# Local attention: softmax division moved ahead of the transposes, weighted values made feature by token, and a new order table

## The chip, the cores and the metric

The kernel runs on one core of one Trainium2 chip. The metric is device time in microseconds (us) of one execution. The core has five engines with in-order instruction queues: TensorE (PE, with its weight loads shown as PEld), VectorE (DVE), ScalarE (ACT), GpSimd (POOL) and SyncE (SP), which only issues DMAs here. They meet through semaphores.

## The reference

Four stages follow each other on an input of 4 sequences of 512 tokens with 128 features: a gated scan with a short convolution, a mixture of eight experts of which one is chosen, grouped-query causal attention, and a stack of six layers of local attention with a gated feed-forward. Only the last stage is touched by the change. One of its layers is, in the reference:

```python
qkv = x @ Wqkv                                   # 16 heads of 64 features
q = l2norm(q) * qs;  k = l2norm(k) * ksc         # then rotary tables with scale
sim = einsum('bhwie,bhwje->bhwij', bq, bk2) * 8  # 32 queries against 64 keys
sim = where(mask, -max, sim)
attn = softmax(sim, -1)
out = einsum('bhwij,bhwje->bhwie', attn, bv2)
return out.reshape(b, n, 1024) @ Wo
...
x = attn_layer(shift_tokens(x), ...) + x
x = ffn_layer(shift_tokens(x), ...) + x
```

Windows have 32 queries, and each window sees its own 32 keys and the 32 before them.

## The kernel before, in words

**Tiling.** The last stage works on chunks of 128 tokens: 6 layers x 4 sequences x 4 chunks = 96 chunks. `Chunk` (class at L531) holds the steps of one. `query(j)` makes 512 columns of queries (j = 0, 1) or keys (j = 2, 3) as [token, feature] in PSUM (L550) and their squares on ACT (L555). `squares` sums these by head (L575). `rotate` multiplies by the two rotary tables on DVE (L563, L567) and adds the products on POOL (L572). `norms` takes the power -0.5 on POOL (L586), and `scale_keys` applies it to the keys on POOL (L593). `turn(j)` transposes four 128x128 blocks on PE (helper at L141) and copies the result to `qT` or `kT` (helper `move`, L529). `values` makes the values (L603, copied by ACT at L607 to a `vr` tile with 65 columns a head, the last of them ones). `spread` issues the DMAs that lay the values of each window's 64 keys into the four `vk` tiles (L617 to L621).

**Scores and softmax.** `mask` writes the mask into the PSUM tile `S` with a bfloat16 matmul (L643), and `scores(g)` adds 32 small matmuls for each half of the heads: 64 rows of features, 32 queries as weights, 64 keys as moving columns (L655). `largest` takes the negative maximum per head and query (L666) and multiplies it by the query's norm (L670). `exponentials(g)` runs four activations of 64 columns each (L679). `flip(g)` transposes half of the exponentials (L689) to `lpT`.

**Weighted values.** `weigh(g)` runs 32 small matmuls for half of the heads with the transposed exponentials as weights (64 keys x 32 queries) and `vk` as 65 moving columns (L702). The result is [token, feature], and its 65th column is the sum of the exponentials. `divide(g)` takes the reciprocal of that column (L711) and multiplies (L713) into `on`. `lift(j)` transposes `on` by four 128x128 blocks (L141, seen as tp_on) and copies it to `oT`. `project` multiplies by the output weights (L729) and adds into the residual (L735).

**Order.** The order of work is written out by hand. `TURN` is a table of (lag, step, arguments). Turn i runs every row on chunk i - lag, so one turn carries one step of each kind, for up to four chunks. `FEED` says ahead of which row of which turn one piece of the feed-forward (a generator with eight pieces per sequence and layer) is put in. `COPIES` says for each of four turns whether a copy out of PSUM goes to DVE ("v") or ACT ("a"). At the end a dependency chains every instruction to the one before it on its engine, so each engine runs exactly this order.

**Buffers.** PSUM has two tiles each of tags "mm" and "tr", and one each (of two banks) of "S" and "o". `qT`, `lp` and `lpT` have one buffer, `vr` has two. A small float32 matmul is one row in the program and two weight loads with two matmuls in the trace.

Of the kernel before, what the change touches and what calls it, by code (L numbers as in the profile page):

```python
# [8 lines left out]
F32 = mybir.dt.float32  # L9
# [6 lines left out]
P = 128  # L16
# [51 lines left out]
def fused(ctx: ExitStack, tc: tile.TileContext, a: dict, out: bass.AP):  # L68
# [387 lines left out]
    with ExitStack() as stage:  # L456
# [21 lines left out]
        vr = [sp.tile([P, 2, HEADS // 2, DH + 1], F32, name=f"vr{i}") for i in range(2)]  # L478
        vk = [sp.tile([P, HEADS // 2, DH + 1], F32, name=f"vk{i}") for i in range(NB)]
        for v in vr:  # L480
            nc.vector.memset(v[:, :, :, DH : DH + 1], 1.0)
# [49 lines left out]
        class Chunk:  # L531


            def __init__(self, n, l, b, c, w, last):
                self.l, self.b, self.c, self.w, self.last = l, b, c, w, last
                self.tag = f"{l}_{b}_{c}"
                self.xs = sA[b][:, c * P : (c + 1) * P]
                self.V = vr[n % 2]
                self.ss = sm.tile([P, 2 * HEADS], F32, tag="ss", name=f"ss{self.tag}")
                self.q = {}  # L540
                self.sq = {}
                self.rot = {}
                self.o = {}
                self.on = {}
# [56 lines left out]
            def values(self, j):  # L601
# [6 lines left out]
                    self.V[:, :, 4 * j : 4 * j + 4, 0:DH],  # L608
# [14 lines left out]
            def window(self):  # L623

                self.qT = wk.tile([P, HEADS // 2, P], F32, tag="qT", name=f"qT{self.tag}", bufs=1)
# [36 lines left out]
            def largest(self):  # L662

                S = self.S.rearrange("p a (s k) -> p a s k", k=KB)
                m = sm.tile([P, HEADS // 2, 2], F32, tag="lm", name=f"lm{self.tag}")
                nc.vector.tensor_reduce(  # L666
                    m.rearrange("p s a -> p a s"), S, AX.X, ALU.max, negate=True
                )
                self.nb = sm.tile([P, HEADS], F32, tag="lnb", name=f"lnb{self.tag}")
                nc.vector.tensor_tensor(  # L670
                    self.nb, m.rearrange("p s a -> p (s a)"), self.rq, ALU.mult
                )
                self.P = wk.tile([P, HEADS, KB], F32, tag="lp", name=f"lp{self.tag}", bufs=1)
                self.pT = wk.tile([P, HEADS // 2, P], F32, tag="lpT", name=f"lpT{self.tag}", bufs=1)

            def exponentials(self, g):

                for i in range(4 * g, 4 * g + 4):
                    nc.scalar.activation(  # L679
                        self.P[:, i, :], self.S[:, i % 2, i // 2 * KB : (i // 2 + 1) * KB], AF.Exp,  # L680
                        bias=self.nb[:, i : i + 1], scale=self.rq[:, i : i + 1],
                    )

# [11 lines left out]
            def weigh(self, g):  # L695
                o = psum("o", f"lo{self.tag}_{g}")[:, :, 0 : 4 * (DH + 1)]
                self.o[g] = o = o.rearrange("p a (s d) -> p a s d", s=4)
                for i in range(4):
                    for r in range(NB):
                        for par in range(2):  # L700
                            lo, to = par * KB, r * QB
                            nc.tensor.matmul(  # L702
                                o[to : to + QB, par, i, :],
                                lhsT=self.pT[lo : lo + KB, 4 * g + i, to : to + QB],
                                rhs=vk[r][lo : lo + KB, 4 * g + i, :], start=True, stop=True,
                            )

            def divide(self, g):
                gt, o = f"{self.tag}_{g}", self.o[g]
                r = sm.tile([P, 2, 4], F32, tag="lr", name=f"lr{gt}")  # L710
                nc.vector.reciprocal(r, o[:, :, :, DH])  # L711
                self.on[g] = wk.tile([P, 512], F32, tag="on", name=f"on{gt}")
                nc.vector.tensor_tensor(  # L713
                    self.on[g].rearrange("p (s a d) -> p a s d", s=4, a=2), o[:, :, :, 0:DH],
                    r[:, :, :, None].to_broadcast([P, 2, 4, DH]), ALU.mult,
                )

            def lift(self, j, engine):

                if j == 0:  # L720
                    self.oT = wk.tile([P, HEADS // 2, P], F32, tag="oT", name=f"oT{self.tag}")
                tp = transposed(chunks(self.on[j]), f"on{self.tag}_{j}")
                move(engine, self.oT[:, 4 * j : 4 * j + 4, :], chunks(tp))

            def project(self):

                y = psum("mm", f"ly{self.tag}")[:, 0:P]
                for j in range(INNER // P):
                    nc.tensor.matmul(  # L729
                        y, lhsT=self.w["o"][:, j, :], rhs=self.oT[:, j, :],  # L730
# [8 lines left out]
        def feedforward(l, b, w):  # L739
# [62 lines left out]
            (3, "exponentials", 3), (1, "scale_keys"), (1, "query", 1), (1, "squares", 0),  # L802
            (2, "turn", 0, "e4"), (1, "rotate", 1), (0, "query", 2), (0, "rotate", 2),
            (3, "flip", 1, "e7"), (2, "mask"), (3, "weigh", 0), (2, "scores", 0),
            (2, "scores", 1), (2, "values", 1), (3, "divide", 0), (3, "weigh", 1), (2, "largest"),
            (1, "squares", 1), (3, "divide", 1), (2, "exponentials", 0), (3, "lift", 0, "e0"),
            (1, "scale_queries"), (2, "values", 0), (0, "query", 3), (0, "squares", 2),
            (1, "window"), (1, "turn", 1, "e5"), (0, "rotate", 3), (3, "lift", 1, "e1"),
            (0, "squares", 3), (0, "query", 0), (2, "spread"), (1, "turn", 3, "e3"),
            (2, "exponentials", 1), (1, "turn", 2, "e2"), (0, "rotate", 0),  # L810
# [158 lines left out]
```

## Time and profile before

| | us |
|---|---|
| median of 3 runs (range) | 2576.98 (2571.02 to 2581.21) |
| the profiled execution's own time | 2581.88 |
| its span | 2580.1 |
| PE busy | 2239.3 (87% of the span) |
| DVE busy | 1923.6 (75%) |
| POOL busy | 1394.2 (54%) |
| ACT busy | 1333.5 (52%) |

The last stage runs from about 735 us to 2555 us of the span. The busy shares above are means over all stages; the last stage has its own. In the profile a row of a group gives the line, engine and operation, the tiles written and read, the count, then busy time and mean duration in ns, and then the idle time of the engine before these instructions with what ended it. Groups overlap where work is pipelined, so busy time is the better figure of the two for a sum. The chain is the sequence of work that ended last, followed back from the end; "issue" in it is time in which an engine waited for nothing that the profile shows.

### The profile page before, as it was taken

Reading aid. Unit: us, or ns where it says so; the run is one execution under the profiler, and the core shown is the slowest. Engines: PE = TensorE matmul, PEld = TensorE weight load, DVE = VectorE, ACT = ScalarE, POOL = GpSimd, SP = SyncE. Lnnn points to the kernel's source line nnn. Section 1 sums busy time; section 2 is a strip of 40 time slices with the busy share of each in tenths; the row PEclk is TensorE's granted clock in tenths of the full one; section 3 lists DMA queues with packets and bytes.
Section 4 is the critical chain, followed back from the end, with each engine's and each line's share of the span. In section 5 each row is a group of like instructions: output and inputs, shape, how many; then the busy total and the mean of one; then the engine's idle time right before and its main releaser. Section 6 shows DMA issues by size and latency. Waiting matters only on the chain.

```text
span 2580.1 us, 80423 instructions
## 1 busy us (share of the span) xinstructions
PE 2239.3 (87%) x33872; PEld 1485.8 (58%) x33968; DVE 1923.6 (75%) x4052; ACT 1333.5 (52%) x3203; POOL 1394.2 (54%) x1002
## 2 busy tenths in 40 slices
PE   3699988888879899989999999998999998989885
PEld 2466644554546566656666666665666665656552
DVE  6444456666759888888888888887888988888863
ACT  1111123233336566666676656666666666666542
POOL 2000011111148777776777777777677777777650
PEclk6699999999999999999999999999999999999997
DMA  6000000000002322232222312222222321212220
GB/s 197 1 1 1 1 1 1 1 1 1 1 7 75 93 60 58 66 92 59 56 66 54 106 51 66 52 71 84 59 60 66 93 66 51 65 50 67 56 55 24
DMA packets 85380, 131.11 MB, mean 51 GB/s; under 512 B 15894, under 2 KB 33564, under 8 KB 84124
## 3 DMA queue, kind: packets, MB, share of 16 engines
q1 hardware_dynamic: 82172, 122.87, 17.6%
q8 instruction: 268, 4.39, 0.7%
q10 hardware_dynamic: 2848, 3.10, 0.4%
q14 instruction: 92, 0.75, 0.1%
HBM read 25.82 MB, written 1.05 MB: 10 GB/s over the span
## 4 chain that ended last, share of the span: by engine, by line
PE 51%; DVE 10%; issue 6%; POOL 1%; ACT 1%; DMA 1%; SPq 0%; POOLq 0%; DVEq 0%; ACTq 0%
PE q L550 10%; PE ly L729 6%; PE lv L603 6%; PE tp_r L141 5%; PE lo L702 5%; PE ls L655 4%; PE tp_on L141 4%; PE fa L768 2%; PE lpt L689 2%; PE fy L778 2%; PE fg L757 2%; DVE lt L563 1%; DVE lt L567 1%; DVE on L713 1%; PE ls L643 1%
## 5 line engine op out<-in xcount | busy, mean ns | idle before, releaser
L572 POOL TENSOR_TENSOR ro<-lt,lt 128x512 f32<-128x512 f32 x384 | 483.5, 1269 | 158.3 <-DVE lt L567 130.0
L679 ACT ACTIVATE lp<-ls,lnb,rn 128x64 f32<-128x64 f32 x1536 | 482.4, 431 | 78.4 <-DVE lnb L670 77.9
L550 PE MATMUL q<-wqkv,sA 128*128 128x512 f32 x768 | 399.9, 603 | 2.8 <-ACT sq L555 1.5
L586 POOL TENSOR_TENSOR rk<-rk,neg_half 128x16 f32<-128x16 f32 x96 | 278.8, 2905 | 147.4 <-DVE rk L582 144.6
L586 POOL TENSOR_TENSOR rn<-rn,neg_half 128x16 f32<-128x16 f32 x96 | 278.9, 2905 | 146.9 <-DVE rn L582 138.5
L563 DVE TENSOR_TENSOR lt<-q,rot 128x512 f32<-128x512 f32 x384 | 262.5, 684 | 72.4 <-ACT sq L555 61.6
L607 ACT COPY vr<-lv 128x512 f32<-128x512 f32 x192 | 113.6, 592 | 388.6 <-PE lv L603 388.2
L555 ACT ACTIVATE sq<-q 128x512 f32<-128x512 f32 x384 | 235.1, 612 | 137.0 <-PE q L550 116.6
L141 PEld LDWEIGHTS tp_r<-ident,ro 128*128 128x128 f32 x1536 | 186.5, 142 | 164.8 <-issue 114.8
L567 DVE TENSOR_TENSOR lt<-q,rot 128x512 f32<-128x512 f32 x384 | 260.8, 679 | 0.0
L575 DVE TENSOR_REDUCE ss<-sq 128x8 f32<-128x512 f32 x384 | 259.6, 676 | 0.0
L702 PEld LDWEIGHTS lo<-vk,lpT 64*32 64x32 f32 x12288 | 143.3, 110 | 187.4 <-issue 153.8
L702 PE MATMUL lo<-vk,lpT 64*32 64x65 f32 x12288 | 183.5, 234 | 59.3 <-issue 36.3
L603 PE MATMUL lv<-wqkv,sA 128*128 128x512 f32 x384 | 220.9, 659 | 3.9 <-DVE lnb L670 2.2
L141 PE MATMUL tp_r<-ident,ro 128*128 128x128 f32 x1536 | 216.5, 274 | 8.9 <-POOL ro L572 7.6
L655 PE MATMUL ls<-kT,qT 64*32 64x64 f32 x12288 | 155.1, 226 | 72.6 <-issue 72.6
L593 POOL TENSOR_TENSOR ro<-ro,rk 128x512 f32<-128x512 f32 x192 | 196.1, 1042 | 7.5
L729 PE MATMUL ly<-oT,lwo 128*128 128x128 f32 x1536 | 188.9, 276 | 1.4 <-DVE lt L567 1.2
L729 PEld LDWEIGHTS ly<-oT,lwo 128*128 128x128 f32 x1536 | 182.2, 193 | 13.1 <-issue 10.6
L655 PEld LDWEIGHTS ls<-kT,qT 64*32 64x32 f32 x12288 | 134.1, 105 | 81.1 <-issue 80.2
L550 PEld LDWEIGHTS q<-wqkv,sA 128*128 128x128 f32 x768 | 127.3, 194 | 69.0 <-issue 49.4
L666 DVE TENSOR_REDUCE lm<-ls 128x16 f32<-128x1024 f32 x96 | 117.2, 1221 | 52.3 <-PE ls L655 51.4
(184 smaller groups left out, 3949.2 us busy)
## 6 DMA issues: line engine op xcount, KB each, us to landing
vk<-vr SPq DMA_DIRECT2D x576, 130.0 KB, 2.4
vk<-vr SPq DMA_DIRECT2D x336, 65.0 KB, 2.0
wqkv<-in_lwqkv_dram SPq DMA_DIRECT2D x6, 1536.0 KB, 7.0
ew<-in_ew_dram SPq DMA_DIRECT2D x16, 256.0 KB, 6.1
lwo<-in_lwo_dram SPq DMA_DIRECT2D x6, 512.0 KB, 8.8
lw<-in_lw_dram SPq DMA_DIRECT2D x6, 341.0 KB, 10.3
cst<-in_cst_dram ACTq DMA_DIRECT2D x1, 1028.0 KB
x_in<-in_x_dram ACTq DMA_DIRECT2D x4, 256.0 KB
```

The lines of the kernel that those rows point to most:

```text
L141: nc.tensor.transpose(tp[:, c * P : (c + 1) * P], i[:, c, :], ident)
L550: nc.tensor.matmul(q, lhsT=self.xs, rhs=self.w["qkv"][:, j * 512 : (j + 1) * 512], start=True, stop=True,)
L563: nc.vector.tensor_tensor(heads(t1), heads(q), cs[:, None, :].to_broadcast([P, 8, DH]), ALU.mult)
L567: nc.vector.tensor_tensor(swapped(t2), swapped(q)[:, :, ::-1, :], sn[:, None].to_broadcast([P, 8, 2, 32]), ALU.mult,)
L572: nc.gpsimd.tensor_tensor(self.rot[j], t1, t2, ALU.add)
L575: nc.vector.tensor_reduce(self.ss[:, j * 8 : j * 8 + 8], heads(self.sq[j]), AX.X, ALU.add)
L586: nc.gpsimd.tensor_tensor(r, r, neg_half.to_broadcast([P, HEADS]), ALU.pow)
L603: nc.tensor.matmul(v, lhsT=self.xs, rhs=self.w["qkv"][:, (4 + j) * 512 : (5 + j) * 512], start=True, stop=True,)
L655: nc.tensor.matmul(S[to : to + QB, par, s, :], lhsT=self.qT[lo : lo + 64, s, to : to + QB], rhs=self.kT[lo : lo + 64, s, to : to + KB], st ...
L679: nc.scalar.activation(self.P[:, i, :], self.S[:, i % 2, i // 2 * KB : (i // 2 + 1) * KB], AF.Exp, bias=self.nb[:, i : i + 1], scale=self. ...
L702: nc.tensor.matmul(o[to : to + QB, par, i, :], lhsT=self.pT[lo : lo + KB, 4 * g + i, to : to + QB], rhs=vk[r][lo : lo + KB, 4 * g + i, :], ...
L729: nc.tensor.matmul(y, lhsT=self.w["o"][:, j, :], rhs=self.oT[:, j, :], start=j == 0, stop=j == INNER // P - 1,)
```

## The change

The exponentials now also give their row sums (`accum_out`). `invert` takes the reciprocals of the sums on DVE, and the new `divide` multiplies the exponentials by them on POOL, before `flip`. `weigh` swaps its operands: `vk` (64 keys x 64 features) is the weights and `lpT` (32 queries) the moving columns. The result is [feature, token], so `lift` is only a copy and its transposes are gone; so are the ones in `vr` and the 65th column. Heads land in `oT` in another order, and the rows of `Wo` are laid out to match on the host. `qT`, `lp` and `lpT` get two buffers, `vr` three. `largest` is split in two rows, and `TURN`, `COPIES` and `FEED` are new.

```diff
-        vr = [sp.tile([P, 2, HEADS // 2, DH + 1], F32, name=f"vr{i}") for i in range(2)]
-        vk = [sp.tile([P, HEADS // 2, DH + 1], F32, name=f"vk{i}") for i in range(NB)]
-        for v in vr:
-            nc.vector.memset(v[:, :, :, DH : DH + 1], 1.0)
+        vr = [sp.tile([P, 2, HEADS // 2, DH], F32, name=f"vr{i}") for i in range(3)]
+        vk = [sp.tile([P, HEADS // 2, DH], F32, name=f"vk{i}") for i in range(NB)]
...
+            def bias(self, engine):
                 self.nb = sm.tile([P, HEADS], F32, tag="lnb", name=f"lnb{self.tag}")
-                nc.vector.tensor_tensor(
-                    self.nb, m.rearrange("p s a -> p (s a)"), self.rq, ALU.mult
-                )
+                engine.tensor_tensor(
+                    self.nb, self.m.rearrange("p s a -> p (s a)"), self.rq, ALU.mult
+                )
...
                         bias=self.nb[:, i : i + 1], scale=self.rq[:, i : i + 1],
-                    )
+                        accum_out=self.sum[:, i : i + 1],
+                    )
+
+            def invert(self, g):
+                r = self.sum[:, 8 * g : 8 * g + 8]
+                nc.vector.reciprocal(r, r)
+
+            def divide(self, g):
+                p = self.P[:, 8 * g : 8 * g + 8, :]
+                nc.gpsimd.tensor_tensor(
+                    p, p, self.sum[:, 8 * g : 8 * g + 8, None].to_broadcast([P, 8, KB]), ALU.mult
+                )
...
             def weigh(self, g):
...
+                if g == 0:
+                    self.o = psum("o", f"lo{self.tag}")
+                for i in range(2 * g, 2 * g + 2):
                     for r in range(NB):
...
+                        for odd in range(2):
+                            s = 2 * i + odd
+                            for par in range(2):
+                                lo, to = par * KB, (par ^ odd) * DH
+                                t0 = i * P + r * QB
+                                nc.tensor.matmul(
+                                    self.o[to : to + DH, odd, t0 : t0 + QB],
+                                    lhsT=vk[r][lo : lo + KB, s, :],
+                                    rhs=self.pT[lo : lo + KB, s, r * QB : (r + 1) * QB],
+                                    start=True, stop=True,
+                                )
+
+            def lift(self, odd, engine):
+
+                if self.oT is None:
+                    self.oT = wk.tile([P, 2, HEADS // 4, P], F32, tag="oT", name=f"oT{self.tag}")
+                move(engine, self.oT[:, odd], chunks(self.o[:, odd]))
...
         TURN = (
...
+            (1, "scale_keys"), (1, "rotate", 1), (1, "window"), (1, "squares", 1),
+            (2, "scores", 1), (2, "values", 1), (0, "query", 2), (3, "flip", 0, "e6"),
+            (2, "largest"), (2, "bias", nc.vector), (0, "rotate", 2), (0, "squares", 2),
+            (3, "spread"), (1, "scale_queries"), (3, "flip", 1, "e7"), (0, "query", 0),
+            (3, "weigh", 0), (0, "rotate", 0), (3, "weigh", 1), (2, "exponentials", 1),
+            (3, "lift", 1, "e1"), (3, "lift", 0, "e0"), (1, "turn", 3, "e3"), (0, "query", 3),
+            (2, "exponentials", 0), (1, "turn", 2, "e2"), (0, "rotate", 3), (0, "squares", 3),
+            (2, "invert", 0), (2, "exponentials", 2), (2, "exponentials", 3), (3, "project"),
+            (1, "turn", 0, "e4"), (0, "squares", 0), (1, "turn", 1, "e5"), (1, "values", 0),
+            (0, "query", 1), (2, "invert", 1), (2, "divide", 0), (1, "mask"), (2, "divide", 1),
+            (1, "scores", 0),
         )
         COPIES = {
-            "e0": "avva",
-            "e1": "aaav",
-            "e2": "vava",
-            "e3": "avav",
-            "e4": "aaav",
-            "e5": "aaav",
-            "e6": "vvvv",
-            "e7": "aaaa",
+            "e0": "aavv",
+            "e1": "vvvv",
+            "e2": "vvva",
+            "e3": "aaaa",
+            "e4": "avaa",
+            "e5": "vvva",
+            "e6": "aaaa",
+            "e7": "aava",
         }
-        FEED = {0: (0, 36), 1: (6,), 2: (0,), 3: (16, 28, 38, 38)}
+        FEED = {1: (2, 38), 2: (6, 9, 21, 23, 33), 3: (30,)}
...
+    wo = np.asarray(i["L1_ffn_Wo"]).reshape(DEPTH, HEADS // 4, 2, 2, DH, D).copy()
+    wo[:, :, 1] = wo[:, :, 1, ::-1].copy()
+    wo = wo.reshape(DEPTH, INNER, D)
```

## The prediction

> **What bounds the kernel now.** I read the page first, for which engine is full.
>
> ```profile
> PE 2239.3 (87%) x33872; PEld 1485.8 (58%) x33968; DVE 1923.6 (75%) x4052; ACT 1333.5 (52%) x3203; POOL 1394.2 (54%) x1002
> q8 instruction: 268, 4.39, 0.7%
> PE 51%; DVE 10%; issue 6%; POOL 1%; ACT 1%; DMA 1%; SPq 0%; POOLq 0%; DVEq 0%; ACTq 0%
> ```
>
> TensorE leads the chain, but these are means over four stages. So I took the busy times of a steady stretch of the last stage: from one piece of the feed-forward (gates, L757) to the same piece 19 sequences, or 76 chunks, later. The columns are span, then busy time (and count) of PE, PEld, DVE, ACT and POOL, the granted clock, DMA share and GB/s.
>
> ```profile
> 961.88:2357.92 1396.04, 1279.84 (x24587) 865.27 (x24663) 1183.42 (x2261) 906.77 (x2167) 1029.38 (x728) 0.98 0.25 66
> ```
>
> That is 18.4 us a chunk: PE works 16.8 of them, DVE 15.6, POOL 13.5, ACT 11.9. PE is the bound, with 1.5 us of idle time a chunk. What ends that idle time stands in the view of waits (who waits for whom: total us, times, longest):
>
> ```profile
> PE ls L655 <- issue: 72.6, 49, 2.5
> PE lo L702 <- issue: 36.3, 37, 2.2
> PE lo L702 <- DVE on L713: 20.9, 18, 5.2
> ```
>
> The largest is "issue", waiting for nothing that the profile shows, and only inside the two bursts of small matmuls. The chain of one turn (start, us, what) shows where:
>
> ```profile
> 1371.77 0.79 PE lo L702 x53
> 1372.56 1.27 PE ls L655 x77
> 1373.84 1.05 PE lv L603 x2
> 1374.89 0.63 PE lo L702 x37
> 1375.52 0.69 issue
> 1376.21 0.43 PE lo L702 x22
> 1376.64 0.58 PE tp_on L141 x4
> ```
>
> Most of these gaps lie within one of a multiple of 256 PE instructions apart (loads and matmuls counted: 511 from the one at 1341.7 to that at 1359.4, 767 to the one at 1376.2). The q8 row above has 268 packets in 4.39 MB, 16.4 KB each; PE's 67,840 instructions make 265 blocks of 256. In the trace the last q8 packet before such a gap mostly starts 2.2 to 2.9 us before the gap ends. So PE runs dry of instructions when it gets through a block faster than the next one comes.
>
> **The change, part by part.** These are the groups, shapes kept apart, that the prices come from:
>
> ```profile
> L141 PE MATMUL tp_on<-ident,on 128*128 128x128 f32 x768 | 128.8, 293 | 14.2 <-DVE oT L529 7.6 <-DVE on L713 3.7 <-issue 2.3
> L702 PE MATMUL lo<-vk,lpT 64*32 64x65 f32 x12288 | 183.5, 234 | 59.3 <-issue 36.3 <-DVE on L713 20.9 <-DMA vk<-vr 1.8
> L655 PEld LDWEIGHTS ls<-kT,qT 64*32 64x32 f32 x12288 | 134.1, 105 | 81.1 <-issue 80.2 <-POOL ro L572 0.4
> L729 PEld LDWEIGHTS ly<-oT,lwo 128*128 128x128 f32 x1536 | 182.2, 193 | 13.1 <-issue 10.6 <-ACT lp L679 2.0 <-ACT oT L529 0.4
> L593 POOL TENSOR_TENSOR ro<-ro,rk 128x512 f32<-128x512 f32 x192 | 196.1, 1042 | 7.5
> L713 DVE TENSOR_TENSOR on<-lo,lr 128x512 f32<-128x512 f32 x192 | 132.8, 692 | 6.7
> L397 ACT ACTIVATION_READ_ACCUMULATOR gp<-gs,gnb 128x1 f32 x128 | 25.3, 198 | 0.0
> ```
>
> *Transposes of `on`.* Eight a chunk go. The chain by line gives them 3.5% of 2580.1 us, 90.3 us, or 0.94 us a chunk on PE: -0.94. Their two copies stay, as copies of the result itself.
>
> *The burst of `weigh`.* The count stays: 128 pairs of load and matmul a chunk. Now 64 pairs take 0.79 us (chain above), 12.3 ns a pair, 1.58 us a chunk. Afterwards a load has 64 columns instead of 32, the matmul 32 moving columns instead of 65, on four 64x64 pieces of the array instead of eight of 64x32. No row has this shape. A load lasts 105 ns at 32 columns and 193 at 128, 0.92 ns a column, so 64 columns hold a piece for 59 ns. Moving columns go by in 0.84 ns (512 take 0.43 us), so 32 take 27 ns. Four pieces at work, loads behind matmuls as in L729 (0.112 us a pair, about one load), make 59/4 = 14.7 ns a pair, 1.88 us a chunk; load and matmul in turn make 86/4 = 21.5 ns, 2.75 us; the pace of the score burst (1.28 us for 128 pairs, 10 ns) makes 1.28. I take 1.88, as full-width rows overlap: +0.30 (-0.30 to +1.17). [...] If the load alone set the old burst too, its price would double to 24.7 ns a pair, +1.58 a chunk, and the forecast below would be 2546 instead of 2423. Against that, the score burst with equal loads runs at 10 ns, so 12.3 is not the load's own limit.
>
> *Where the bursts lie.* Before, 516 PE instructions come in one stretch of 4.0 us (half of `weigh`, both `scores`, a value matmul, half of `weigh`): wherever a block begins, one lies wholly inside. After, by the instruction order, the 256 of the scores and the 256 of `weigh` stand apart. Between them are 28 instructions of about 3.5 us on one side (value, two `query`, two `flip`) and 80 of about 6.5 us on the other. A block is too fast only if it begins within 28 instructions of where a burst does: 2 x 56/256 = 0.44 a chunk, at 0.8 us (half of the typical 1.6 us gap) 0.35 us. Now it is 108.9/96 = 1.13. So -0.78 (0 to -1.13). [...]
>
> *PE's waits for `on`, `oT` and `vk`.* 20.9 + 7.6 + 3.7 + 1.8 = 34.0 us, 0.35 a chunk, go with `on`. What PE waits for next is the copy of `lpT`, two rows later on the same engines. I keep half: -0.18 (-0.35 to 0).
>
> *`spread`.* Its ten DMAs a chunk (eight at a sequence's start) are 0.54 us apart on SP and land 2.0 to 2.4 us after issue, so 8 us after the last `weigh` frees `vk`. SP holds nothing else but the next layer's weights. Before, it waited for values made in the same turn; after, those are a turn old and the next `weigh` is a turn minus the burst away, 15 us. No cost.
>
> *DVE.* Two L713 (0.61 start to start) and two reciprocals (0.23) go, two reciprocals of 128x8 come (0.2 each), 14 of 32 copies fall to it instead of 13 (+0.15): 15.6 - 1.7 + 0.4 + 0.15 = 14.5 us. Now `invert` waits on DVE for exponentials; behind it stand the next chunk's norms, rotation and squares, 1.9 us, which POOL and then PE wait for. DVE has 2.3 us to spare for it in a turn of 16.8.
>
> *ACT.* 16 sums are read out: the L397 row says 198 ns busy, but in the timeline the next activation starts 0.09 us after it. 12 exponentials now take 3.67 us, so 16 take 4.9 and grow by 1.5 (0 to 3.2). ACT: 11.9 + 1.5 - 0.1 = 13.3 us. The one place it can reach PE is `S`: the next mask waits for the last exponential. Scores' end, maximum 1.22, bias 0.69, exponentials 6.4, some seven copies and squares of 0.5 between, mask and scores 1.7: 13.5 us, hidden in the turn, even with 1.7 more.
>
> *POOL.* Two divisions in L593's shape, 1.0 us each start to start: 13.5 + 2.0 = 15.5 us. They lie beside PE's 16.8, but the cover is thin: 1.3 us. Behind `divide` on POOL stands `scale_keys` (2.9 + 2.0 us), which the key transposes on PE wait for; they come half a turn later. If POOL falls behind, its time is the turn.
>
> *Second and third buffers* cost nothing. The ramp, about 2400 to 2555 us, I leave as it is.
>
> Sum a chunk: -0.94 + 0.30 - 0.78 - 0.18 = -1.60, a turn of 16.8 us. Times 96: -154 us. The profiled execution took 2581.9, so 2428; it lies 4.9 above the median of the runs, so **2423**.
>
> **The rivals.**
> *POOL and DVE set the turn.* POOL's waits now (L586 on DVE 144.6 and 138.5 us, L572 on DVE 130.0) are 4.3 us a chunk. They speak for a queue that is ahead and should shrink as PE speeds up, but in-order queues that wait for each other keep some. With half: 15.5 + 2.15 = 17.7, 0.7 saved, 2510.
> *Faster still.* No fetch gap left and the burst at 10 ns: 16.8 - 0.35 - 0.60 = 15.8, just over POOL's 15.5: 2332. For it: the score burst does run so. Against: everything must fit.
> *Slower: the new burst.* Its two row halves write the same PSUM bank, which they did not before[...]. No row here has such a pair. If they go one after the other, two pieces work at a time: 86/2 = 43 ns a pair, 5.5 us, +3.9 a chunk in place of +0.30: a turn of 20.4, 2769. It decides from 27 ns a pair on, 3.5 us a chunk, where it eats the 1.9 us saved. Against it: the halves write different partitions.
> *No change in effect* can't be: the transposes do go.
>
> **How the numbers follow.** The forecast 0.58 (its own range 2370 to 2475, from the ends of burst and fetch), POOL and DVE 0.20, faster still 0.12, the burst 0.10. The measurement can tell about 0.5%, 13 us, from no change; of the POOL case 0.02 and of the burst case 0.02 lie within. Faster 0.88, same 0.04, slower 0.08. The range 2340 to 2520 leaves out the burst (0.10), half of the faster case and a little of the POOL case.
>
> **What would show it.** Right: a turn near 16.8 us in the steady stretch; no tp_on; lo pairs at 13 to 17 ns; issue gaps at lo and ls under 50 us together; POOL above 90% busy. Wrong: lo at over 27 ns a pair; issue gaps still near 109 us; PE idle on POOL's keys or on `lpT`, with POOL or DVE full.

## The result, and the profile after

The changed kernel takes **2550.24 us** (median of 4 runs, 2543.93 to 2559.03) against 2578.06 for the kernel before on the same chip: a ratio of 0.9898, with a 95% interval of 0.9862 to 0.9934. It is 1.0% faster. The forecast was 6% (2423 us), and its range ended at 2520, so forecast and range were both wrong. The likeliest rival, "POOL and DVE set the turn" at 2510, was nearer, and the sections below show that something like it happened, but with ACT in POOL's place. Nearest of all was 2546, but by luck: that number belongs to a burst of 24.7 ns a pair, and the burst runs at 17.

The page of the profiled execution (2559.03 us, 9 above the median; span 2557.2), in the places shown of before:

```profile
PE 2226.0 (87%) x33200; PEld 1463.6 (57%) x33200; DVE 1821.2 (71%) x3882; ACT 1459.8 (57%) x4715; POOL 1584.1 (62%) x1194
q8 instruction: 263, 4.31, 0.7%
PE 44%; DVE 8%; ACT 7%; issue 4%; DMA 3%; SPq 2%; POOL 2%; ACTq 0%; POOLq 0%; DVEq 0%
```

PE is as full as before. In the chain, PE and "issue" have less, while ACT has 7% instead of 1%. The steady stretch over the same 76 chunks (span, then busy time and count of PE, PEld, DVE, ACT and POOL, then the granted clock):

```profile
943.30:2302.30 1359.00, 1261.32 (x24057) 842.48 (x24056) 1100.61 (x2129) 1007.74 (x3364) 1179.95 (x880) 0.98 0.26 67
```

Divided by 76 this is a turn of 17.88 us: PE 16.6, DVE 14.5, ACT 13.3, POOL 15.5. The loads of DVE, ACT and POOL are those forecast, to 0.1 us; the turn is 0.49 us shorter, where 1.60 was forecast. PE's idle time went from 1.53 us a chunk (18.37 - 16.84) to 1.29 (17.88 - 16.60). The waits of PE say what that idle time now is (who waits for whom: total us, times, longest):

```profile
PE ls L640 <- ACT lp L679: 38.5, 46, 1.3
PE ly L735 <- ACT oT L527: 37.6, 26, 2.3
PE ls L652 <- issue: 20.1, 12, 4.0
PE lo L718 <- issue: 15.4, 15, 1.8
PE lo L718 <- DMA vk<-vr: 14.2, 11, 6.0
```

"Issue" at the bursts fell from 108.9 us to 35.5, as forecast. But 76.1 us of waiting for ACT are new: the mask waits for the last exponential, and the output projection waits for ACT's copy of the result. Neither was on PE's list before with more than a microsecond. The groups that the forecast priced:

```profile
L718 PE MATMUL lo<-lpT,vk 64*64 64x32 f32 x12288 | 210.9, 222 | 33.2 <-issue 15.4 <-DMA vk<-vr 14.2 <-DVE lpT L527 2.8
L735 PE MATMUL ly<-oT,lwo 128*128 128x128 f32 x1536 | 197.4, 284 | 39.5 <-ACT oT L527 37.6 <-DVE oT L527 1.0 <-ACT lp L679 0.9
L679 ACT ACTIVATION_READ_ACCUMULATOR lp<-ls,lnb,rn 128x1 f32 x1536 | 355.9, 232 | 0.0
```

The new burst has 210.9 us against 183.5 before: +27.4 us, or +0.29 a chunk. The read-outs of the sums are 1536, 16 a chunk.

Where do the two waits on ACT come from? The timeline shows it in one place that comes back in every sequence (start, us, engine, line, operation; in brackets the idle time ahead and what ended it). First ACT, in the turn whose mask stood at 1187.7 us:

```profile
1193.92 0.40 ACT L679 ACTIVATE lp<-ls,lnb,rn 128x64 f32<-128x64 f32 x1
...
1196.30 0.58 ACT L527 COPY oT<-lo 128x512 f32<-128x512 f32 x1 [0.72 <-DVE oT L527]
...
1197.74 0.42 ACT L679 ACTIVATE lp<-ls,lnb,rn 128x64 f32<-128x64 f32 x1
1198.03 0.22 ACT L679 ACTIVATION_READ_ACCUMULATOR lp<-ls,lnb,rn 128x1 f32 x1
1198.12 0.42 ACT L679 ACTIVATE lp<-ls,lnb,rn 128x64 f32<-128x64 f32 x1
...
1202.23 0.27 ACT L679 ACTIVATION_READ_ACCUMULATOR lp<-ls,lnb,rn 128x1 f32 x1
...
1214.58 0.58 ACT L527 COPY oT<-lo 128x512 f32<-128x512 f32 x1 [2.73 <-DVE oT L527]
```

An exponential with its read-out is 0.38 us from start to start (1197.74 to 1198.12), and without pause the last 12 fill ACT for 4.8 us. The next mask comes at 1202.55, having waited 0.89 us for them. The loop from mask to mask took 14.8 us here (1187.73 to 1202.55). Behind it, DVE in the following turn, and PE's output projection:

```profile
1204.07 0.69 DVE L560 TENSOR_TENSOR lt<-q,rot 128x512 f32<-128x512 f32 x1 [1.29 <-ACT sq L552]
...
1205.27 0.28 DVE L122 BATCH_NORM_STATS2 st_f<-fn 128x6 f32<-128x128 f32 x1
...
1206.99 0.87 DVE L124 TENSOR_TENSOR rs_f<-mv_f,eps 128x4 f32<-128x4 f32 x1
...
1213.87 0.68 DVE L527 COPY oT<-lo 128x512 f32<-128x512 f32 x1
```

```profile
1202.55 0.59 PE L640 MATMUL ls<-mask_h,ident_h 128*128 128x512 bf16 x2 [0.89 <-ACT lp L679]
...
1208.93 2.07 PE L718 MATMUL lo<-lpT,vk 64*64 64x32 f32 x128
1210.92 0.70 PE L141 MATMUL tp_r<-ident,ro 128*128 128x128 f32 x4
...
1212.32 0.60 PE L141 MATMUL tp_r<-ident,ro 128*128 128x128 f32 x4
1215.22 3.39 PE L735 MATMUL ly<-oT,lwo 128*128 128x128 f32 x16 [2.29 <-ACT oT L527]
```

DVE idles 1.29 us for ACT's squares, which stood behind the exponentials. Then it works without a gap for 11 us, 2.5 of them the feed-forward's statistics (1205.27 to 1207.78), before it copies its half of the result at 1213.87, 2.9 us after the burst that made it ended. ACT's half starts 0.71 us later, 0.03 us after DVE's has ended, and the profile names DVE's copy as what released it. It is so in all 48 chunks in which the two engines share the copies: both read one PSUM tile, and ACT starts 0.03 to 0.04 us after DVE has ended, never before. (Two copies by DVE, one right behind the other, overlap by 0.08 us.) Nor does DVE's first rotation product of a `q` tile start before ACT's square of it has ended, 384 times out of 384 (at least 0.03 us behind it), and these two share no other tile. PE stands still for 2.29 us.

### The profile page after: what moved, and what is told of

Its sections match the earlier page's. It is cut to its first block, busy times and chain, and to the rows that moved or that the text cites. A ratio compares the mean times of both kernels' runs of the same rounds, so it can differ in the third digit from the quotient of the medians.

```text
span 2557.2 us, 80510 instructions
## 1 busy us (share of the span) xinstructions
PE 2226.0 (87%) x33200; PEld 1463.6 (57%) x33200; DVE 1821.2 (71%) x3882; ACT 1459.8 (57%) x4715; POOL 1584.1 (62%) x1194
## 4 chain that ended last, share of the span: by engine, by line
PE 44%; DVE 8%; ACT 7%; issue 4%; DMA 3%; SPq 2%; POOL 2%; ACTq 0%; POOLq 0%; DVEq 0%
PE q L547 9%; PE lo L718 6%; ACT lp L679 5%; PE lv L600 5%; PE tp_r L141 5%; PE ls L652 4%; PE ly L735 4%; DMA vk<-vr 3%; PE fa L774 2%; PE fg L763 2%; PE fy L784 2%; PE lpt L700 2%; DVE lt L560 2%; DVE lt L564 1%; PE ls L640 1%
## 5 line engine op out<-in xcount | busy, mean ns | idle before, releaser
L679 ACT ACTIVATE lp<-ls,lnb,rn 128x64 f32<-128x64 f32 x1536 | 598.6, 430 | 15.0 <-DVE lnb L669 9.2
L547 PE MATMUL q<-wqkv,sA 128*128 128x512 f32 x768 | 406.7, 612 | 14.5 <-DVE lt L564 8.1
L679 ACT ACTIVATION_READ_ACCUMULATOR lp<-ls,lnb,rn 128x1 f32 x1536 | 355.9, 232 | 0.0
L691 POOL TENSOR_TENSOR lp<-lp,lsum 128x512 f32<-128x512 f32 x192 | 200.0, 1042 | 108.4 <-DVE rk L579 60.9
L718 PEld LDWEIGHTS lo<-lpT,vk 64*64 64x64 f32 x12288 | 196.7, 137 | 108.1 <-ACT lpT L527 53.7
L604 ACT COPY vr<-lv 128x512 f32<-128x512 f32 x192 | 119.9, 624 | 215.0 <-PE lv L600 215.0
L718 PE MATMUL lo<-lpT,vk 64*64 64x32 f32 x12288 | 210.9, 222 | 33.2 <-issue 15.4
L141 PE MATMUL tp_r<-ident,ro 128*128 128x128 f32 x1536 | 229.7, 281 | 7.1 <-POOL ro L590 3.9
L735 PE MATMUL ly<-oT,lwo 128*128 128x128 f32 x1536 | 197.4, 284 | 39.5 <-ACT oT L527 37.6
L600 PE MATMUL lv<-wqkv,sA 128*128 128x512 f32 x384 | 212.4, 636 | 1.3 <-DVE sA L741 1.3
```

Of the source, the lines that this page charges most:

```text
L141: nc.tensor.transpose(tp[:, c * P : (c + 1) * P], i[:, c, :], ident)
L547: nc.tensor.matmul(q, lhsT=self.xs, rhs=self.w["qkv"][:, j * 512 : (j + 1) * 512], start=True, stop=True,)
L600: nc.tensor.matmul(v, lhsT=self.xs, rhs=self.w["qkv"][:, (4 + j) * 512 : (5 + j) * 512], start=True, stop=True,)
L679: nc.scalar.activation(self.P[:, i, :], self.S[:, i % 2, i // 2 * KB : (i // 2 + 1) * KB], AF.Exp, bias=self.nb[:, i : i + 1], scale=self. ...
L718: nc.tensor.matmul(self.o[to : to + DH, odd, t0 : t0 + QB], lhsT=vk[r][lo : lo + KB, s, :], rhs=self.pT[lo : lo + KB, s, r * QB : (r + 1) ...
L735: nc.tensor.matmul(y, lhsT=self.w["o"][:, j, :], rhs=self.oT[:, j % 2, j // 2, :], start=j == 0, stop=j == INNER // P - 1,)
```

## The experiments

Each edit is against the changed kernel unless it is called an edit of the kernel before. Times are medians of 4 runs; ratios are to the kernel before, run beside them. Its own median differs between these sets (2571 to 2579 us), so a difference of two medians from different sets can be off by some 7 us. All waits come from one trace of each kernel.

**1. The read-outs, and the drain** (the last chunks, where the work thins out). Three kernels. The first takes the sums off ACT.

```diff
-                        accum_out=self.sum[:, i : i + 1],
...
-                nc.vector.reciprocal(r, r)
+                nc.vector.tensor_scalar(r, self.P[:, 8 * g : 8 * g + 8, WIN], 1.0, None, ALU.add)
```

> The changed kernel without the row sums (no accum_out; the reciprocal is replaced by adding 1 to one exponential of each head, an operation of the same size on DVE that still waits for the same exponentials; the division multiplies by that, so the output is not the reference's). Theory A, the 16 read-outs a chunk lengthen the exponentials by 1.5 us a turn, and the squares, the mask and, over DVE, the copies behind them on ACT are late for PE: the waits of PE for lp (38.5 us) and for oT (37.6 us) fall by more than half, and the time goes from 2550 to 2450 to 2490. Theory B, DVE with the feed-forward's statistics in one turn of four is late by itself: the waits for oT stay above 30 us and the time stays at 2530 to 2550.

The second writes the last layer's output one turn later, behind that turn's spread on SP, and the third has both edits.

```diff
-            nc.sync.dma_start(out[b].rearrange("(c p) d -> p c d", p=P), n)
+            finished.append((b, n))
...
                     getattr(made[i - lag], what)(*of)
+                    if what == "spread":
+                        finished[:] = done + finished
+                        write()
```

> The changed kernel with the output DMA of each sequence issued behind the next turn's spread instead of at once. Theory C, the output DMA waits on SP for the last layernorm (77.6 us in all) and the spread behind it is late for weigh (PE waited 14.2 us for vk): that wait goes to under 3 us and the time falls by 12 to 20 us, to 2530 to 2538. Theory D, the last two sequences are long because of the longer way of one chunk through exponentials, sums, division and spread: less than 5 us.

> Both edits of the two runs before it (so the row sums are left out and the output is not the reference's). A and C: the gains add, 2435 to 2475. If only C holds 2530 to 2538, if neither 2545 to 2555.

Without read-outs: 2523.69 us, ratio 0.981 (0.9795 to 0.9825), 26.6 us less than the changed kernel by the medians, 23 by the ratios. Output later: 2544.45, ratio 0.989 (0.9871 to 0.9908), not to be told from the changed kernel by its time; theory C's 12 to 20 us did not come. Both: 2520.47, ratio 0.9789 (0.9767 to 0.981), far from the 2435 to 2475 expected. PE's waits without read-outs:

```profile
PE q L547 <- DVE sA L740: 25.4, 42, 1.0
...
PE q L547 <- DVE lt L564: 20.4, 25, 1.6
...
PE ly L734 <- ACT oT L527: 12.3, 20, 1.8
```

The mask's wait for the exponentials is down from 38.5 us to 0.5, and the wait for the copies to a third, but PE now waits for DVE: for the residual (sA) and the rotation products (lt), 45.8 us at the queries. So the read-outs were not hidden, but they are worth far less than the 127 us that lie between forecast and measurement. The time falls between the two theories' ranges: A had the mechanism and too high a price.

**2. The read-outs in the kernel before.** An edit of the kernel before: it makes the same sums on ACT and doesn't use them.

```diff
                         bias=self.nb[:, i : i + 1], scale=self.rq[:, i : i + 1],
+                        accum_out=self.sum[:, i : i + 1],
```

> The kernel before with accum_out on its exponentials, the sums unused. If a read-out costs its 0.09 us wherever it stands, 16 x 96 of them cost up to 140 us: 2640 to 2720. If it costs only where the next step on ACT is waited for, as theory A says of the new order, the old order, which has the mask 8 rows behind the last exponentials and ACT at 12 of 18.4 us a chunk, hides most of it: 2575 to 2600.

2610.46 us, ratio 1.0149 (1.0124 to 1.0175): +39 us, 0.4 us a chunk for 1.5 us of ACT's time, which lies between the two expectations. Even in the old order, in a mean turn of 18.4 us and with ACT at 52% of the span, a quarter of it comes through. ACT's share of the span says little about whether it has room.

**3. The copy of the result.** One letter: in the second turn of each sequence both halves are copied by ACT, so that neither stands behind DVE's statistics.

```diff
-            "e1": "vvvv",
+            "e1": "vavv",
```

> After, but in the second turn of each sequence both copies of the result (oT) are made by ACT; in after one half is ACT's and one DVE's, both read the same PSUM tile, and the profile of after has PE's output projection (ly) waiting 37.6 us (26 times) for ACT's half, which itself stands behind DVE's. Theory A (DVE, late with the feed-forward's statistics in that turn, holds ly through ACT's copy, and the PE gap of about 2.3 us also slows the matmuls behind it, 3.39 us for 16 instead of 1.79): some 20 such turns at 2.3 + 1.6 us, less 0.6 us for the longer ACT queue: ly's wait for oT under 10 us and a time of 2480 to 2530 us. Theory B (DVE's lateness only reappears at the next thing it makes, q, lt or the statistics): ly's wait falls but others on DVE or ACT rise by as much; 2540 to 2560 us.

2525.73 us, ratio 0.9803 (0.9775 to 0.983): 24.5 us less than the changed kernel, as theory A had it.

```profile
PE ls L652 <- issue: 34.1, 19, 4.3
PE ls L640 <- ACT lp L679: 27.1, 34, 1.4
...
PE lo L718 <- issue: 18.9, 17, 1.7
...
PE ly L735 <- DVE lt L564: 15.6, 14, 1.2
...
PE ly L735 <- ACT oT L527: 2.7, 5, 1.4
```

The projection's wait for ACT's copy went from 37.6 to 2.7 us. Part of it comes back as a wait for DVE's rotation products (15.6), and part as "issue" at the bursts, which rose from 35.5 to 53.0 us.

**4. Two pieces of the array instead of four.** The two row halves write straight instead of crossed, which leaves two of four 64x64 pieces in use.

```diff
-                                lo, to = par * KB, (par ^ odd) * DH
+                                lo, to = par * KB, par * DH
...
-    wo[:, :, 1] = wo[:, :, 1, ::-1].copy()
```

> After, but the two row halves of the array write the same half of the partitions of their result instead of crossed ones, so that only two 64x64 pieces can be at work at one time. Prices from before's rows (59 ns load, 27 ns matmul of a piece): load and matmul in turn 86/2 = 43 ns a pair, 5.5 us a chunk; loads behind matmuls 59/2 = 29.5 ns, 3.8 us; after has 15.6 ns, 2.00 us. Theory A (four pieces at once is what makes the burst short): 3.8 to 5.5 us a chunk, the time 2550 + 96 x 1.8 to 3.5, 2720 to 2890 us. Theory B (the pace is set by PE's issue of instructions, not by the pieces): 2.0 to 2.4 us a chunk and 2550 to 2590 us.

2661.14 us, ratio 1.0332 (1.03 to 1.0365): +111 us. The group of the burst and one instance of it:

```profile
L718 PE MATMUL lo<-lpT,vk 64*64 64x32 f32 x12288 | 388.8, 221 | 14.4 <-DMA vk<-vr 12.7 <-DVE lpT L527 1.0 <-ACT lpT L527 0.3
```

```profile
1256.16 3.92 PE L718 MATMUL lo<-lpT,vk 64*64 64x32 f32 x128
```

That is 388.8 / 12288 = 31.6 ns a pair, against 17.2 (210.9 / 12288) with four. So with two pieces in use a pair takes 1.84 times as long as with four, which speaks for four at work at once. If so, a pair keeps its piece for some 63 ns (2 x 31.6) by estimate, close to the 59 that the forecast estimated for the load alone. The burst grew by 178 us, but the time by 111: a longer burst on PE leaves the others time, and the wait for ACT's copy fell from 37.6 to 9.1 us. At this pace "issue" is not among the three largest waits of the new burst, the third of which is 0.3 us; the changed kernel had 15.4 us of it. Both expectations missed the time; A had the pace.

**5. The bursts apart, in the kernel before.** Two edits of its order table alone (with the row numbers in `FEED` moved along), to test what the forecast said of the gaps. The first moves half of `weigh` ahead of a query and the other half behind a key or query transposition (`turn`).

```diff
-            (3, "exponentials", 3), (1, "scale_keys"), (1, "query", 1), (1, "squares", 0),
+            (3, "exponentials", 3), (1, "scale_keys"), (3, "weigh", 0), (1, "query", 1),
...
-            (1, "window"), (1, "turn", 1, "e5"), (0, "rotate", 3), (3, "lift", 1, "e1"),
+            (1, "window"), (1, "turn", 1, "e5"), (3, "weigh", 1), (3, "divide", 1),
+            (0, "rotate", 3), (3, "lift", 1, "e1"),
...
```

> Before, with nothing changed but the order table: the two halves of weigh are put apart from the scores (first half ahead of the query behind it, second half with its division behind the second turn), so that no 512 small PE instructions come in one stretch. Theory A (the 'issue' gaps at the bursts are instruction fetch and cost what they last): issue gaps at lo and ls together fall from 108.9 us to under 50 us, and the time by 50 to 80 us, to 2490 to 2525 us. Theory B (gaps go, but PE then waits for ACT and DVE by as much): gaps under 50 us and a time of 2555 to 2600 us. Theory C (the gaps have nothing to do with where the bursts lie): gaps stay near 109 us and the time near 2575 us.

2796.9 us, ratio 1.0867 (1.083 to 1.0905). PE's waits:

```profile
PE tp_on L141 <- DVE on L713: 137.0, 101, 4.0
PE lo L702 <- DVE lpT L529: 70.0, 73, 1.0
PE lo L702 <- DMA vk<-vr: 43.9, 121, 0.6
...
PE ls L655 <- issue: 4.3, 4, 1.5
```

The gaps are gone, 4.3 us instead of 108.9, but the steps moved now wait for what they read, and the time is far outside all three expectations. The second puts the scores first and both halves of `weigh` behind two value and two query steps, and uses the divisions later.

```diff
-            (3, "flip", 1, "e7"), (2, "mask"), (3, "weigh", 0), (2, "scores", 0),
-            (2, "scores", 1), (2, "values", 1), (3, "divide", 0), (3, "weigh", 1), (2, "largest"),
...
+            (3, "flip", 1, "e7"), (2, "mask"), (2, "scores", 0), (2, "scores", 1),
+            (2, "values", 1), (2, "largest"), (1, "squares", 1), (2, "exponentials", 0),
+            (1, "scale_queries"), (2, "values", 0), (0, "query", 3), (0, "squares", 2),
+            (3, "weigh", 0), (3, "divide", 0), (3, "weigh", 1), (3, "divide", 1), (1, "window"),
...
```

> Before, computation unchanged, with the scores ahead and both halves of weigh behind two value and two query steps, and the divisions' results used later than in the first attempt at this, so that the 256 instructions of the scores and the 256 of weigh stand apart by some 3.5 us. Theory A (the gaps are instruction fetch, and are worth what they last): issue gaps at lo and ls fall from 108.9 us to under 55 us and the time to 2500 to 2535 us. Theory B (gaps go, but new waits for on or oT take their place): gaps under 55 us and 2560 to 2650 us.

2666.72 us, ratio 1.0346 (1.0311 to 1.0381). The gaps are 11.6 us:

```profile
PE lo L702 <- DVE on L713: 134.4, 96, 2.0
...
PE ls L655 <- issue: 8.2, 5, 1.9
PE lo L702 <- issue: 3.4, 5, 1.0
```

One wait, the second half of `weigh` for the first half's division, takes 134.4 us, and the time is above both expectations. So in two orders out of two the gaps went with the stretch of 512 small instructions, as the forecast had it. These two leave a rival: PE waits more in them, and the gaps may have gone for that. The next experiment speaks against it. What the gaps are worth alone could not be shown, since each order brought waits of its own that were larger.

**6. The new computation in the old order.** The old table as far as its steps exist, with the sums' reciprocals and the divisions right behind the exponentials.

```diff
...
+            (3, "exponentials", 3), (3, "invert", 1), (3, "divide", 1), (1, "scale_keys"),
+            (1, "query", 1), (1, "squares", 0), (2, "turn", 0, "e4"), (1, "rotate", 1),
+            (0, "query", 2), (0, "rotate", 2), (3, "flip", 1, "e7"), (2, "mask"),
+            (3, "weigh", 0), (2, "scores", 0), (2, "scores", 1), (2, "values", 1),
+            (3, "weigh", 1), (2, "largest"), (2, "bias", nc.vector), (1, "squares", 1),
...
```

> After, but the parts stand in the order table of before as far as they exist (invert and divide right behind the exponentials, weigh where it was) with the copies' engines of before. Theory A (the saving of after comes mostly from regrouping the bursts): the gaps at lo and ls stay near 109 us (over 80), and the time is 2590 to 2640 us, slower than before, as the divided exponentials now wait for all sums ahead of the transposes. Theory B (the saving is the transposes that went): 2540 to 2570 us with gaps near 109 us.

3079.41 us, ratio 1.1956 (1.1923 to 1.199).

```profile
PE lpt L700 <- POOL lp L691: 224.4, 83, 6.3
...
PE ls L652 <- issue: 60.1, 53, 2.6
...
PE lo L718 <- issue: 20.4, 40, 0.9
```

The gaps at both bursts are 80.5 us, as A had it, though this kernel waits more than any other here: it has the long stretch, and the gaps stay. The time is far above both theories, as the transposes of the exponentials wait 224.4 us for POOL's division. In the old table this change is a loss; the new order is no extra of it.

**7. What sets the turn, once both waits are gone.** Three kernels. Both copies on ACT and the output later:

> After with two edits: both copies of the result on ACT in the second turn of each sequence (which brought 24.5 us), and the last layer's output written one turn later on SP, so that the spread of the values no longer stands behind it (5.8 us alone). Theory A (the two losses are apart, in different layers and queues): 2550.2 - 24.5 - 5.8, about 2520 us (2514 to 2526). Theory B (the drain is held by something else once the copy is moved): 2525 us, as with the copy alone.

The copies moved, and no divisions on POOL:

> After with both copies on ACT in the second turn, and the two divisions on POOL left out (1.0 us each, 2 us a chunk; the exponentials are transposed undivided, so the output is not the reference's). Theory A (as predicted, POOL's 15.5 us lie beside PE and DVE): 2515 to 2530 us, no change from 2525.7. Theory B (POOL's queue is what DVE and PE wait for through the keys and rotation): 2 us a chunk less on POOL brings 0.3 to 0.8 us a chunk, 2450 to 2500 us.

The copies moved, the output later and no read-outs:

> After with three edits: no sums read out on ACT (1 plus a column of the exponentials stands in for the row sums, output not the reference's), output written later, and both copies on ACT in the second turn. Without the copy edit the other two gave 2520.5 us. Theory A (read-outs and copy order are separate losses): a further 15 to 25 us, 2495 to 2505 us. Theory B (both shift the same wait, ACT behind a late DVE; once one is gone DVE's feed-forward statistics set the turn): 2510 to 2522 us.

2517.06 us, ratio **0.9768** (0.9735 to 0.9801), for copies and output: faster than both kernels. 2512.05, ratio 0.9742 (0.9713 to 0.9771), without the divisions. 2511.99, ratio 0.9744 (0.9711 to 0.9777), for all three.

The last number is the telling one. Without read-outs some 25 us were gained, and as much by the copy, but with the copy moved and the output later, leaving out the read-outs too brings only 5 us more, within the spread of the runs. They are not two losses. They are two places of one chain: exponentials on ACT, squares behind them, rotation on DVE, statistics, copy of the result, projection on PE. PE's waits in that kernel:

```profile
PE q L547 <- DVE lt L564: 25.7, 25, 4.1
...
PE ls L652 <- issue: 23.5, 20, 3.4
PE q L547 <- DVE sA L740: 21.2, 33, 1.0
PE lo L717 <- issue: 18.7, 18, 1.6
```

They are DVE's, for rotation products and for the residual, and again "issue" at the bursts, 42.2 us together. PE's two waits for ACT are down to 2.7 us, for the copy.

The divisions on POOL cost nothing in the steady stretch: from the 9th projection to the 80th a chunk takes 17.52 us with and without them. They cost in the last 16 chunks, 309.9 against 292.9 us. So POOL's cover holds, as forecast, until the work thins out at the end.

**8. The statistics moved.** What was left was why DVE is late in that turn. The feed-forward's first piece is called behind the copies of the result instead of ahead of the scores.

```diff
-        FEED = {1: (2, 38), 2: (6, 9, 21, 23, 33), 3: (30,)}
+        FEED = {1: (22, 38), 2: (6, 9, 21, 23, 33), 3: (30,)}
```

> After, but the feed-forward's first piece (its transposes on PE, their copy on ACT and the statistics on DVE, 2.5 us there in one stretch) is called in the second turn of each sequence behind the copies of the result instead of ahead of the scores' second half; the next piece stays where it was. Theory A (the statistics, standing ahead of DVE's copy of the result in the one turn that has them, are what makes it and so ACT's copy and the output projection late): PE's wait for the copies falls from 37.6 to under 10 us, and the time to 2515 to 2535 us, as with the copies moved. Theory B (DVE is late in that turn because ACT's squares come late behind the exponentials with their read-outs, 1.3 us of idle time ahead; the statistics only fill): the wait falls by less than half and the time is 2540 to 2560 us.

The other run has this edit beside the copies and the output.

> After with three edits: the statistics later, as in the run beside it, both copies on ACT in that turn, and the last layer's output written one turn later (the last two alone gave 2517.1). Theory A (copies and statistics are two ways to take away the same wait): 2510 to 2522 us. Theory B (DVE's lateness in that turn still costs PE something after the copies have moved, 15.6 us of waits for rotation products among it): 2490 to 2508 us.

2550.5 us, ratio 0.988 (0.9842 to 0.9917), and 2519.82 us, ratio 0.9771 (0.9742 to 0.9801): neither can be told from the same kernel without the edit. PE's waits in the first:

```profile
PE q L547 <- DVE lt L564: 21.1, 27, 1.6
...
PE lv L600 <- DVE lt L564: 11.4, 21, 0.6
...
PE tp_r L141 <- ACT fn L750: 10.6, 16, 0.9
PE ly L735 <- ACT oT L527: 5.0, 7, 1.8
```

Theory A was right on the wait (37.6 to 5.0 us) and wrong on the time: 43.1 us of other waits for DVE and ACT stand in its place; of these the changed kernel has 8.1 us, for rotation products at the queries. "Issue" at the bursts rose too, from 35.5 to 51.8 us. The statistics do hold up the copy, but DVE's work in that turn is the same in any order, and PE meets it elsewhere. The edit that helped took a copy off DVE in that turn; the one that only reordered DVE did not.

## Why the prediction was wrong

By its own steps, a chunk:

| step | forecast, us | found, us |
|---|---|---|
| transposes of `on` | -0.94 | gone |
| burst of `weigh` | +0.30 | +0.41 from start to start (1.99 against 1.58); +0.29 by the busy time of the group |
| other work of PE | 0 | about +0.3 (what is left: PE's busy time fell 0.24 instead of 0.64) |
| "issue" gaps at the bursts | -0.78 | -0.76 (73.4 us / 96) |
| other waits of PE | -0.18 | about +0.5 |
| the turn | -1.60 | -0.49 |

*The step that failed* is that ACT's and DVE's new work lies beside PE's. The sum has no term for it, and lets PE's other waits shrink by 0.18 us a chunk, half of those for `on`, `oT` and `vk`. They grew by about 0.5 instead. "Hidden in the turn" of ACT's loop, and DVE's "2.3 us to spare", were both set against the mean turn of 16.8 us. And `S` was called "the one place" where ACT can reach PE: the copy of the result to `oT`, over which 37.6 us came, was taken to be out of the way with `on`.

The turns are not alike. From one mask to the next, the four turns of a sequence take 15.1, 18.8, 19.8 and 17.9 us on average in the changed kernel (9th to 81st mask), since the feed-forward's work on PE, ACT and DVE is put into some of them. In the shortest, the loop of scores and exponentials (14.8 us where it is shown above; 13.5 forecast) fills the turn, and the mask waits. In the next, DVE has 2.5 us of statistics that no other turn has, more than all the spare time that the mean gave it. It is this second turn that pays: without read-outs it takes 16.8 us, with the copies moved 17.1. The shortest stays at 15.1 and 15.2, though the mask no longer waits for exponentials without read-outs, and the third grows to 21.4 and 20.6.

The experiments on read-outs and copies show what that costs: about 25 us by either, and 38 by both together with the output's edit. That is less than a third of the 127 us between forecast and measurement. The rest is in the rows on PE's work, in the drain, and in waits that no edit here took away: with copies and output moved a chunk still takes 17.4 us from the 9th projection to the 80th (changed kernel 17.9, before 18.4).

*A second size was off in PE's work.* The transposes went, yet PE's busy time fell by 0.24 us instead of 0.64. The burst is part of it: it takes 1.99 us from start to start where it is shown above, and 1.88 was forecast. Some 0.05 us is only in the record: the page of before has 96 matmuls fewer than weight loads, one mask matmul a chunk that its trace lacks, and the page of after has them all. The busy time of the key and query transposes (tp_r) rose from 216.5 to 229.7 us over the run, that of the projection from 188.9 to 197.4, of the query matmuls from 399.9 to 406.7, of the feed-forward's fa from 73.5 to 78.0. Part of it lies behind waits, in stretches with a granted clock of 0.50: five of the projection's (last section) take 5.6 us more together than they would at 2.05 us each, and with the copies moved the projection is back at 190.7. Part seems to be that a burst now runs into the four transposes of queries or keys, which in the instance above take 0.70 us there and 0.60 elsewhere, where before those of `on` stood behind it. These rows overlap in time, so the rest is not divided further, and its cause stays open.

*The drain* was left out. In the last layer SP holds the output's DMA too, not just "the next layer's weights". It waits for the last layer norm, with the spread of the values behind it:

```profile
SPq L802 <- DVE ln L130: 77.6, 3, 28.3
```

That gave the 14.2 us of PE's wait for `vk`; with the output one turn later it is 0.4, while the wait for `lpT` at the same burst grows from 2.8 to 6.4. The last 16 chunks took 299.8 us before and 307.5 after, while a saving of 1.6 us a chunk had been counted for them as well. With the copies moved they are 309.9, and 300.9 with the output later as well; the total doesn't tell this gain from nothing.

*What held:* that the "issue" gaps go with the long stretch of small instructions, and their fall (35.5 us in the changed kernel, "under 50"), though what the fall freed was taken up by waits. In the traces, counting PE's loads, matmuls and semaphore instructions (and the mask matmul that the trace of before lacks), the gaps of over 0.5 us at the bursts follow each other at multiples of 256, to within 3 in all 79 distances before and to within 1 in all 23 after; the last q8 packet ahead starts 2.2 to 3.0 us before the gap ends. Experiments 5 and 6 fit this: 4.3 and 11.6 us of gaps where the long stretch was broken up, 80.5 where it was kept. The size of the fall may be in part luck: with the copies moved, where PE waits less, the gaps are back at 53.0 us, and at 47.2 with the output moved too. The pace of the burst: lo pairs at 17.2 ns by the group, 15.5 from start to start in the instance shown (1.99 us / 128), "13 to 17". The slow rival's price, 43 ns a pair, did not come; it was an estimate with no row behind it. POOL is at 87% in the steady stretch (1179.95 / 1359.00), where "above 90%" was for a turn of 16.8. The turn of 16.8 us itself exists: in the kernel with copies and output moved, some sequences take 67.0 us for four chunks.

*Of the three signs of a wrong forecast named in advance* none came. Two looked at the burst and the gaps, which were right, and "PE idle on POOL's keys or on `lpT`" was the wrong place to look: PE came to idle on the exponentials and the result's copies.

## What to carry to other kernels

Spare time of a queue has to be taken in the turn where the work is, and not in the mean turn: in a schedule of unlike turns, set each engine's load in each turn against that turn's length, and look for the turn that holds the periodic extra work. When work goes from the bounding engine to two others, follow the chain across them (here exponentials, squares, rotation, copy, projection), since here lateness added up along it and a reordering only moved the wait. Two copies out of one PSUM tile by two engines were a serial pair here, 48 times out of 48; where one engine is late, try giving both to the other (24.5 us here).

## What the hardware showed beside this

- Behind some PE gaps the granted clock was 0.50. The 16 matmuls of the projection take 1.95 us with no gap ahead, but 3.39 behind the gap of 2.29 us above: the trace has a granted clock of 0.50 there, from 1215.67 us for 3.41 us. Of the 14 such stretches behind a gap of over 1.6 us, nine took 2.05 us at a clock of 1.00, and five took 2.49 to 3.59 with the clock at 0.50 for 1.0 to 3.3 us of them. What decides it was not tested. From the 9th projection to the 80th the clock stands at 0.50 for 55 us in the kernel before, 44 in the changed one and 17 with copies and output moved. By estimate, if half of such time is lost at a clock of 0.50, up to 14 of the 33 us that those two edits save in this stretch may be the clock's.
- With copies and output moved, the two longest gaps of "issue" in the steady stages, the only ones over 2.2 us, fall where the next layer's weights are loaded: 3.75 us up to 1411.3 and 3.95 us up to 1960.6. From 1400 to 1412 us and from 1950 to 1961 us the DMA engines move 278 and 284 GB/s, against a mean of 52 over the span, and the weights' five DMAs are among them. Whether the transfer makes these gaps longer was not tested.
- An activation with its sum read out is 0.38 us from start to start at 128x64, against 0.29 without: the read-out costs 0.09 us, although its row shows 232 ns busy.
